# Fetching the rows of expert blocks up to 12 blocks ahead, in two rates, instead of 4 ahead at one a block

## The chip, the core and the metric

The kernel runs on one core of one Trainium2 chip. The metric is the device time in microseconds of one execution, lower is better. TensorE (PE) multiplies matrices and transposes, VectorE (DVE) and ScalarE (ACT) do elementwise work and empty PSUM, GpSimd (POOL) does elementwise work and issues the indirect DMAs, SyncE (SP) issues most of the other DMAs. Each engine works through its own queue in order, and engines wait for one another by semaphores.

## The reference

A transformer block on `x` of 8 x 256 tokens with 256 features, in float32:

```python
x = x + _layernorm(_L0_attn_ref(_layernorm(x), w_qkv, w_o, qn_g, qn_b, kn_g, kn_b))
x = x + _layernorm(_L0_ffn_ref(_layernorm(x), gate_w, w_gate, w_up, w_down, shgate_w, ...))
```

The attention has 16 query heads and 4 key heads of 128, a norm on queries and keys, rotary positions and a causal softmax. The second half, which the change touches, is a mixture of experts:

```python
logits = jnp.einsum('td,ed->te', xf, gate_w)            # 2048 tokens, 8 experts
weights, indices = jax.lax.top_k(softmax(logits), 2)    # two experts a token
g = jnp.einsum('td,edh->teh', xf, w_gate)
u = jnp.einsum('td,edh->teh', xf, w_up)
h = silu(g) * u                                         # 176 hidden units an expert
out = jnp.einsum('teh,ehd,te->td', h, w_down, combine)  # combine: normalised weights
out = out + sigmoid(xf @ shgate_w)[:, None] * (silu(xf @ shw_gate) * (xf @ shw_up) @ shw_down)
```

The last line is a shared expert with 352 hidden units for every token.

## The kernel before, in words

**First half.** Attention runs in a hand-written order over 8 sequences. Tokens are held as 16 tiles of 128. As each tile's attention is done, its normalised rows `xf` are written to a DRAM array `xf_rows`, and its two experts are found. This ends at about 590 us.

**Blocks.** The 2048 x 2 pairs of token and expert are sorted by expert into blocks of 128 rows. There are `NB` = 39 blocks. `load["src"]` holds the row numbers of each block.

**The loop.** `for s in range(CLOSED)` (L1311) is a software pipeline, one slot for each block. In slot `s` the kernel works on four blocks at different stages, in this order on TensorE:

- `turn_block(s)` transposes the fetched rows (`xt`, L1142); VectorE copies the result to `xT` (L1144).
- `open_block(s - 1)` multiplies by the gate and up weights (`gu`, L1158); ScalarE applies silu (`slb`, L1163), VectorE multiplies (`h`, L1165). The expert's number is in a register, loaded for 20 blocks at a time (L1149).
- `close_block(s - 3)` multiplies by the down weights (`py`, L1183); ScalarE copies (`yb`, L1188) and SyncE writes the rows to the DRAM array `ys` (L1189).
- `turn_hidden(s - 2)` transposes the hidden units (`ht`, L1173); ScalarE copies (`hTb`, L1175).

From slot 20 on each slot also holds one step of the shared expert (`gus`, L284, or `sd`, L304), by `fill(1)`.

**Fetches.** `fetch(b)` (L1130) is an indirect DMA on POOL's queue: 128 rows of 1 KB from `xf_rows` into a buffer `xb`. Before, `AHEAD` = 4 blocks are fetched ahead of the loop and slot `s` fetches block `s + 4`. `xb` has five buffers, so the fetch of block `b` waits for the transposes of block `b - 5`.

**Collects.** `collect(i, k)` (L1192) is also an indirect DMA on POOL's queue. It gathers the k-th expert's rows of token tile `i` out of `ys` into `got`. A plan made ahead of the loop puts collects, `combine`, `deviation_of_two` and `leave_tile` into slots. `FULL` = 11, 15, 19, ... 39 is the number of blocks that must be written before a pair of tiles may be collected, so collects begin at slot `FULL[0] + 4` = 15. `combine(i)` (L1202) adds on VectorE what was collected; `deviation_of_two` (L1222) is a small power on POOL (`rstd_d`, L1225) that waits for VectorE and stands in POOL's queue among fetches and collects.

**`places`** (L1086) spreads over slots 2 to 10 some VectorE work (L1103, L1107, L1111) that finds where each token's rows will lie in `ys`.

Of the kernel before, what the change touches and what calls it, by code (L numbers as in the profile page):

```python
# [9 lines left out]
F32 = mybir.dt.float32  # L10
# [9 lines left out]
P = 128  # L20
B, S, HID = 8, 256, 256
# [14 lines left out]
NB = T * TOPK // P + E - 1  # L36
# [6 lines left out]
FULL = [end * TOPK + E - 1 for end in ENDS]  # L43
# [5 lines left out]
def block_kernel(  # L49
# [310 lines left out]
    def fill(n):  # L360
        for f in todo[:n]:
            f()
        del todo[:n]
# [632 lines left out]
    fw = ctx.enter_context(tc.tile_pool(name="fw", bufs=3))  # L996
# [31 lines left out]
    def table():  # L1028

        pn = ps_tr.tile([P, NP], F32, tag="tr", name="total")  # L1030
        nc.tensor.matmul(
            pn, lhsT=ones, rhs=count.rearrange("p g e -> p (g e)"), start=True, stop=True
        )
        n = fc.tile([P, NP], U32, name="n")
        nc.vector.tensor_scalar(n, pn, P - 1.0, None, ALU.add)
        nc.vector.tensor_scalar(n, n, P.bit_length() - 1, None, ALU.logical_shift_right)
        upto = nb[:, E:]
        nc.vector.tensor_copy(upto, n)

        end = fc.tile([P, NP], F32, name="end")  # L1040
        nc.vector.tensor_tensor_scan(
            end, upto, nb[:, :NP], 0.0, ALU.add, ALU.subtract
        )

        off = fc.tile([P, NP], F32, name="off")
        nc.vector.tensor_sub(off, upto, end)
        nc.vector.tensor_add(off, off, lift.rearrange("p g e -> p (g e)"))
        nc.vector.tensor_sub(jump[:, : NP - 1], off[:, 1:], off[:, : NP - 1])

        past = fc.tile([P, NP], F32, name="past")  # L1050
        more = fc.tile([P, 1], F32, name="more")
        nc.vector.scalar_tensor_tensor(
            past, end, part, jump, ALU.is_le, ALU.mult, accum_out=more
        )
        pickT = fc.tile([P, P], F32, name="pickT")
        nc.vector.tensor_scalar(pickT, aside, more, None, ALU.is_equal)
        load["pickT"], load["upto"], load["off"] = pickT, upto, off

    def rows_of():
        ps = ps_tr.tile([P, NB], F32, tag="tr", name="pickp")  # L1060
        nc.tensor.transpose(ps, load["pickT"][:NB, :], ident[:NB, :NB])
        pick = fc.tile([P, NB], F32, name="pick")
        nc.vector.tensor_copy(pick, ps)
        load["pick"] = pick

    def sources():
        ps = ps_tr.tile([P, NB], F32, tag="tr", name="whose")
        nc.tensor.matmul(ps, lhsT=member, rhs=load["pick"], start=True, stop=True)
        src = fc.tile([P, NB], U32, name="src")
        nc.vector.tensor_copy(src, ps)  # L1070
        load["src"] = src
        load["row"] = ps_tr.tile([1, NB], F32, tag="tr", name="row")
        nc.tensor.matmul(load["row"], lhsT=part, rhs=load["pick"], start=True, stop=True)

    def experts():

        er = fc.tile([1, NB], I32, name="er")
        nc.vector.tensor_copy(er, load["row"])
        nc.vector.tensor_scalar(er, er, (T // P).bit_length() - 1, None, ALU.logical_shift_right)
        ei = fc.tile([1, -(-NB // LB) * LB], I32, name="ei")  # L1080
        if ei.shape[1] > NB:
            nc.vector.memset(ei, 0)
        nc.vector.tensor_scalar_min(ei[:, :NB], er, E - 1)
        load["ei"] = ei
# [41 lines left out]

    state = {}
    AHEAD = 4

    def fetch(b):  # L1130
        x_b = fw.tile([P, HID], F32, tag="xb", name=f"xb_{b}", bufs=AHEAD + 1)
        nc.gpsimd.indirect_dma_start(
            out=x_b, out_offset=None, in_=xf_rows,
            in_offset=bass.IndirectOffsetOnAxis(ap=load["src"][:, b : b + 1], axis=0),
        )
        state["x", b] = x_b

    def turn_block(b):
        tr = ps_tr.tile([P, KC, P], F32, tag="tr", name=f"xt_{b}")
        x_b = state.pop(("x", b))  # L1140
        for c in range(KC):
            nc.tensor.transpose(tr[:, c, :], x_b[:, c * P : (c + 1) * P], ident)  # L1142
        xT = fw.tile([P, KC, P], F32, tag="xT", name=f"xT_{b}")
        nc.vector.tensor_copy(xT, tr)  # L1144
        state["xT", b] = xT

    def open_block(b):
        if b % LB == 0:
            _, state["at"] = nc.values_load_multi_w_load_instructions(  # L1149
                load["ei"][:, b : b + LB],  # L1150
                engines=[mybir.EngineType.PE], min_val=0, max_val=E - 1,
                skip_runtime_bounds_check_because="an expert's number, at most 7",
            )
        xT = state.pop(("xT", b))
        gu = ps_mm.tile([P, 2 * HE], F32, tag="mm", name=f"gu_{b}")
        e = state["at"][b % LB]
        for c in range(KC):
            nc.tensor.matmul(  # L1158
                gu, lhsT=xT[:, c, :], rhs=wgu_sb.rearrange("p c (e h) -> p c e h", e=E)[:, c, bass.ds(e, 1), :],
                start=(c == 0), stop=(c == KC - 1),  # L1160
            )
        sl = fw.tile([P, HE], F32, tag="slb", name=f"slb_{b}")
        nc.scalar.activation(sl, gu[:, :HE], AF.Silu)  # L1163
        h = hs[b % 2]
        nc.vector.tensor_mul(h[:, :HE], sl, gu[:, HE:])  # L1165
        state["h", b] = h
        state["e", b] = e
# [81 lines left out]
    def first_share(i):  # L1249
        y = state["y", 0, i]  # L1250
        nc.scalar.activation(y, y, AF.Copy, scale=share[:, i, 0:1])
# [23 lines left out]
    with tc.manual_schedule():  # L1275
        table()
        fill(2)
        rows_of()
        sources()
        for b in range(AHEAD):  # L1280
            fetch(b)
        experts()
        fill(2)

        CLOSED = NB + 3
        plan = {}

        def at(slot, f, *args):
            plan.setdefault(slot, []).append(lambda: f(*args))

        for g in range(G - 3):
            s = FULL[g] + 4
            for j in range(2 * TOPK):
                at(s + j, collect, 2 * g + j // TOPK, j % TOPK)
            for j in range(2):
                at(s + 3 + 2 * j, combine, 2 * g + j)
                at(s + 7 + j, leave_tile, 2 * g + j)
            at(s + 6, deviation_of_two, 2 * g + 1)

        for g in range(G - 3, G - 1):  # L1300
            s = FULL[g] + 4
            for j in range(2 * TOPK):
                at(s + j // TOPK, collect, 2 * g + j // TOPK, j % TOPK)
        g, s = G - 3, FULL[G - 3] + 4
        for j in range(2):
            at(s + 3 + j, combine, 2 * g + j)
            at(s + 6 + j, leave_tile, 2 * g + j)
        at(s + 5, deviation_of_two, 2 * g + 1)
        finding = places()
        LATE = 6  # L1310
        for s in range(CLOSED):  # L1311
            if s + AHEAD < NB:
                fetch(s + AHEAD)
            if s < NB:
                turn_block(s)
            if s == 0:
                fill(1)
            if 0 <= s - 1 < NB:
                open_block(s - 1)
            if 0 <= s - 3 < NB:  # L1320
                close_block(s - 3)
            if 0 <= s - 2 < NB:
                turn_hidden(s - 2)
            if 2 <= s < G + 3:
                next(finding)
            calm = s >= FULL[G - 3] + 7
            if calm:
                for f in plan.pop(s, ()):
                    f()

            if 20 <= s and len(todo) > LATE:
                fill(1)
            for f in plan.pop(s, ()):
                f()
        for f in plan.pop(CLOSED, ()):
            f()
        assert not plan and len(todo) == LATE
        z = NTILES - 4
        for j in range(2 * TOPK):
            collect(z + 2 + j // TOPK, j % TOPK)  # L1340
        fill(2)
        for j in range(2):
            combine(z + j)
        deviation_of_two(z + 1)
        fill(2)
        first_share(z + 2)
        fill(1)
        first_share(z + 3)
        leave_elsewhere(z)
        for j in range(2, 4):  # L1350
            both_shares(z + j)
        fill(1)
        for j in range(2, 4):
            combine_last(z + j)
        for j in range(2, 4):
            leave_last_tile(z + j, (nc.scalar, nc.sync)[j - 2])
        assert not todo
# [47 lines left out]
```

## Time and profile before

| | |
|---|---|
| median of 3 runs | 754.91 us (753.23 to 756.32) |
| profiled execution | 755.46 us |
| its span, first to last instruction | 753.7 us |
| mean granted TensorE clock | 0.988 |
| TensorE busy | 720.3 us, 96% of the span |
| POOL busy | 396.5 us, 53% of the span |
| first fetch issued | 591.59 us |
| last fetch issued | 707.51 us |
| first and last collect issued | 632.23 us, 740.45 us |

Times inside the profiled execution are counted from the start of its span. A row of the timeline gives start, duration, engine, line, operation, output and inputs, and in brackets how long the engine had been idle and what ended that. "issue" means that the profile shows nothing that it waited for. [...]

### The profile page before, as it was taken

How to read it: one execution, taken by the hardware profiler on the slowest of the kernel's cores; microseconds unless marked ns; L12 is line 12 of the kernel's file. 1: busy time of each engine (PE TensorE's matmuls, PEld its weight loads, DVE VectorE, ACT ScalarE, POOL GpSimd, SP SyncE). 2: the span in 40 equal slices, each digit the busy share in tenths (PEclk: the TensorE clock that was granted, in tenths of full speed). 3: DMA queues.
4: the chain of work that ended last, by engine and by line, in shares of the span. 5: the costliest groups of instructions: out<-in, count | busy, mean ns of one | idle time of the engine just before them, and what ended most of it. 6: DMA issues, size and time to landing. Idle time of an engine off the chain costs nothing.

```text
span 753.7 us, 11344 instructions
## 1 busy us (share of the span) xinstructions
PE 720.3 (96%) x3448; PEld 533.8 (71%) x3448; DVE 548.0 (73%) x1464; ACT 459.3 (61%) x1448; POOL 396.5 (53%) x455
## 2 busy tenths in 40 slices
PE   7779999999999999999999999999999899899994
PEld 4446677777777777777777777777887677777773
DVE  4788778788888978896897889678746473354464
ACT  2688877677777767776776767677741333332332
POOL 5568467365546636573654657365212535455423
PEclk9899999999999999999999999999999999999998
DMA  9400000000000000000000000002303133344322
GB/s 309 153 2 1 0 1 8 1 7 1 8 1 7 1 8 8 0 8 1 7 2 8 1 9 7 1 9 70 92 9 91 56 102 119 93 124 116 111 88 76
DMA packets 26915, 32.36 MB, mean 43 GB/s; under 512 B 2980, under 2 KB 23048, under 8 KB 26856
## 3 DMA queue, kind: packets, MB, share of 16 engines
q1 hardware_dynamic: 22752, 21.94, 9.0%
q0 software_dynamic: 3408, 9.31, 4.6%
q8 instruction: 28, 0.46, 0.3%
q10 hardware_dynamic: 696, 0.40, 0.2%
q14 instruction: 31, 0.25, 0.1%
HBM read 22.33 MB, written 9.31 MB: 42 GB/s over the span
## 4 chain that ended last, share of the span: by engine, by line
PE 87%; DVE 4%; ACT 4%; POOL 2%; issue 1%; DMA 1%; SPq 0%; POOLq 0%; DVEq 0%; ACTq 0%
PE qkv L412 20%; PE o L639 15%; PE sc L543 10%; PE av L620 10%; PE gu L1158 6%; PE tp L602 5%; PE py L1183 5%; PE tq L507 4%; PE gus L284 4%; PE sd L304 2%; PE xt L1142 1%; PE ht L1173 1%; ACT qn L454 1%; PE in L768 1%; ACT w_qkv L247 1%
## 5 line engine op out<-in xcount | busy, mean ns | idle before, releaser
L412 PE MATMUL qkv<-w_qkv,xnT 128*128 128x512 f32 x384 | 183.3, 603 | 0.0
L480 POOL TENSOR_TENSOR t<-qn,sg_q 128x256 f32<-128x256 f32 x128 | 118.4, 945 | 54.7 <-ACT qn L454 53.0
L445 POOL TENSOR_TENSOR rstds<-ves,nhalf 128x4 f32<-128x4 f32 x80 | 93.6, 1170 | 74.2 <-DVE ves L436 73.9
L639 PE MATMUL o<-wo_sb,oT 128*128 128x256 f32 x512 | 125.1, 384 | 0.0
L454 ACT ACTIVATE qn<-qkv,rstds 128x128 f32<-128x128 f32 x320 | 91.7, 372 | 33.8 <-POOL rstds L445 33.6
L412 PEld LDWEIGHTS qkv<-w_qkv,xnT 128*128 128x128 f32 x384 | 71.6, 194 | 54.5 <-issue 50.0
L571 ACT ACTIVATE ex<-sc,nmx 128x128 f32<-128x128 f32 (+1 forms) x256 | 105.3, 432 | 5.1 <-DVE nmx L560 4.2
L543 PE MATMUL sc<-kT,q 128*128 128x256 f32 (+1 forms) x512 | 99.7, 328 | 2.5 <-DVE q L517 2.5
L620 PE MATMUL av<-pT,v 128*128 128x256 f32 (+1 forms) x320 | 98.6, 422 | 0.6 <-ACT pT L607 0.6
L639 PEld LDWEIGHTS o<-wo_sb,oT 128*128 128x128 f32 x512 | 91.4, 190 | 9.3
L555 DVE TENSOR_TENSOR sc<-sc,mask 128x256 f32<-128x256 f32 (+1 forms) x96 | 49.3, 514 | 43.1 <-PE sc L543 42.8
L543 PEld LDWEIGHTS sc<-kT,q 128*128 128x128 f32 x512 | 74.7, 191 | 6.0 <-ACT w_qkv L247 2.7
L507 PEld LDWEIGHTS tq<-ident,t 128*128 128x128 f32 x320 | 40.4, 143 | 47.3 <-issue 35.1
L607 ACT COPY pT<-tp 128x512 f32<-128x512 f32 x96 | 57.2, 595 | 24.1 <-PE tp L602 24.1
L560 DVE TENSOR_REDUCE nmx<-sc 128x2 f32<-128x512 f32 (+1 forms) x96 | 66.2, 689 | 2.8
L602 PEld LDWEIGHTS tp<-ident,ex 128*128 128x128 f32 x384 | 47.6, 141 | 25.8 <-issue 12.9
L620 PEld LDWEIGHTS av<-pT,v 128*128 128x128 f32 x320 | 59.0, 190 | 9.2 <-ACT pT L607 1.3
L468 DVE TENSOR_TENSOR t<-qn,cg_q 128x512 f32<-128x512 f32 x64 | 57.9, 904 | 8.5 <-ACT qn L454 8.2
L430 ACT ACTIVATE sq<-qkv 128x512 f32<-128x512 f32 x80 | 48.2, 603 | 22.5 <-PE qkv L412 13.1
L436 DVE TENSOR_REDUCE ves<-sq 128x4 f32<-128x516 f32 x80 | 54.5, 682 | 8.2 <-ACT sq L430 8.0
L602 PE MATMUL tp<-ident,ex 128*128 128x128 f32 x384 | 58.5, 274 | 1.4 <-DVE xnT L402 0.7
L631 ACT COPY oT<-av 128x512 f32<-128x512 f32 x64 | 37.7, 590 | 35.6 <-PE av L620 35.6
(198 smaller groups left out, 1230.1 us busy)
## 6 DMA issues: line engine op xcount, KB each, us to landing
ys<-yb SPq DMA_DIRECT2D x39, 128.0 KB
w_qkv<-in_wqkvT SPq DMA_DIRECT2D x6, 512.0 KB
x_all<-in_x SPq DMA_DIRECT2D x8, 256.0 KB
wo_sb<-in_woT SPq DMA_DIRECT2D x1, 2048.0 KB
xf_rows<-xf SPq DMA_DIRECT2D x16, 128.0 KB
out<-yo SPq DMA_DIRECT2D x14, 128.0 KB
wgu_sb<-in_wg SPq DMA_DIRECT2D x2, 704.0 KB
wgu_sb<-in_wu SPq DMA_DIRECT2D x2, 704.0 KB
```

The costliest lines, as they stand in the source:

```text
L412: nc.tensor.matmul(ps.rearrange("p h d -> p (h d)"), lhsT=seqs[b]["xnT"][t][:, c, :], rhs=w_qkv[g][:, c, :], start=(c == 0), stop=(c == KC ...
L445: nc.gpsimd.tensor_tensor(rstd, now.pop(("ve", b, j)), nhalf, ALU.pow)
L454: nc.scalar.activation(qn[:, h, :], ps[:, h, :], AF.Copy, scale=rstd[:, h : h + 1])
L468: nc.vector.tensor_mul(t1, now["qn", b, j], cg[s][:, t : t + 1, :].to_broadcast([P, REP, D]))
L480: nc.gpsimd.tensor_tensor(t2[:, :, lo : lo + HD], qn[:, :, hi : hi + HD], sg[s][:, t : t + 1, lo : lo + HD].to_broadcast([P, REP, HD]), AL ...
L507: nc.tensor.transpose(tr[:, h, :], t1[:, h, :], ident)
L543: nc.tensor.matmul(sc[:, h, :], lhsT=seqs[b]["qT"][g][:, r0 + h, t * P : (t + 1) * P], rhs=seqs[b]["kT"][:, g, :w], start=True, stop=True,)
L560: nc.vector.tensor_reduce(out=nm, in_=now["sc", b, u], axis=AX.X, op=ALU.max, negate=True)
L571: nc.scalar.activation(ex[:, h, :], sc[:, h, :], AF.Exp, bias=nm[:, h : h + 1], accum_out=rs[:, h : h + 1],)
L602: nc.tensor.transpose(tr[:, c, :], ex[:, h, k * P : (k + 1) * P], ident)
L620: nc.tensor.matmul(now["av"][:, r0 : r0 + nh, :].rearrange("p h q -> p (h q)"), lhsT=seqs[b]["v"][:, k, g * D : (g + 1) * D], rhs=pT[:, k ...
L639: nc.tensor.matmul(now["o", b, t], lhsT=seqs[b]["oT"][h // REP, t][:, h % REP, :], rhs=wo_sb[:, h, :], start=(h == 0), stop=(h == H - 1),)
```

## The change

`AHEAD` stays at 4 and the first four fetches stay ahead of the loop. The buffers of `xb` grow from 5 to 13 (`MOST + 1`). The slot in which a block is fetched now comes from a formula. With `QUIET` = `FULL[0] + 3` = 14, blocks 4 to 24 are put at three in two slots, and later ones at four in seven slots. So slot 0 fetches blocks 4 and 5, slot 10 block 19 only and slot 9 block 18, slot 14 block 25, slot 15 block 26, slot 17 block 27; the last ones are block 36 in slot 33, block 37 in slot 35 and block 38 in slot 36. The most that a fetch runs ahead is 11 slots, the least 2.

```diff
     AHEAD = 4
+    MOST = 12
+    QUIET = FULL[0] + 3
+
+    def slot_of_fetch(b):
+
+        early = QUIET * 3 // 2
+        n = b - AHEAD
+        return n * 2 // 3 if n < early else QUIET + (n - early) * 7 // 4
+
 
     def fetch(b):
-        x_b = fw.tile([P, HID], F32, tag="xb", name=f"xb_{b}", bufs=AHEAD + 1)
+        x_b = fw.tile([P, HID], F32, tag="xb", name=f"xb_{b}", bufs=MOST + 1)
         nc.gpsimd.indirect_dma_start(
...
         for s in range(CLOSED):
-            if s + AHEAD < NB:
-                fetch(s + AHEAD)
+            for b in range(AHEAD, NB):
+                if slot_of_fetch(b) == s:
+                    assert s <= b <= s + MOST
+                    fetch(b)
             if s < NB:
                 turn_block(s)
```

## The prediction

> **What bounds the kernel now.** I read the busy table first, then the windows of the second half, then the list of waits, then the timeline.
>
> ```profile
> PE 720.3 (96%) x3448; PEld 533.8 (71%) x3448; DVE 548.0 (73%) x1464; ACT 459.3 (61%) x1448; POOL 396.5 (53%) x455
> ...
> PE 87%; DVE 4%; ACT 4%; POOL 2%; issue 1%; DMA 1%; SPq 0%; POOLq 0%; DVEq 0%; ACTq 0%
> ```
>
> TensorE is busy for 96% of the span and carries 87% of the chain. A change that leaves its work alone can only act through its gaps. The changed loop starts its first fetch at 591.59 us, so only the last 162 us matter. Windows of 10 us (columns: PE, PEld, DVE, ACT, POOL, clock, DMA share, GB/s):
>
> ```profile
> 590.00:600.00 10.00, 7.67 (x36) 5.65 (x37) 2.78 (x11) 1.33 (x4) 6.58 (x7) 1.00 0.25 73
> 610.00:620.00 10.00, 10.00 (x50) 7.70 (x49) 7.69 (x21) 3.86 (x12) 3.83 (x5) 1.00 0.34 105
> 630.00:640.00 10.00, 10.00 (x49) 7.64 (x48) 2.38 (x7) 2.89 (x9) 6.53 (x7) 1.00 0.44 131
> 640.00:650.00 10.00, 7.88 (x29) 5.69 (x28) 3.77 (x10) 3.07 (x10) 5.68 (x6) 0.83 0.38 115
> ```
>
> TensorE is full except in two of these rows. In 590 to 600 it waits for the first fetch and for its own load of the experts' numbers (1.57 us). In 640 to 650 it loses 2.1 us, and the granted clock is 0.83. Who waited for whom from 590 us on (total, times, longest):
>
> ```profile
> POOL rstd_d L1225 <- DVE mv_d L1220: 25.2, 6, 5.5
> POOL xb L1132 <- PE xt L1142: 21.2, 15, 2.8
> PE xt L1142 <- DMA xb<-xf_rows,src: 0.4, 1, 0.4
> ```
>
> The third line is the one for this change: TensorE waited for a fetched block once, 0.4 us, at the first block. The second is POOL waiting for TensorE to free one of five buffers. No row has VectorE waiting for a `got`. The POOL timeline shows the pace:
>
> ```profile
> 599.40 0.94 POOL L1132 DMA_INDIRECT xb<-xf_rows,src  x1 [0.30 <-issue]
> 600.65 0.95 POOL L1132 DMA_INDIRECT xb<-xf_rows,src  x1 [0.30 <-PE xt L1142]
> ...
> 622.45 0.95 POOL L1132 DMA_INDIRECT xb<-xf_rows,src  x1 [1.54 <-PE xt L1142]
> ...
> 632.23 0.95 POOL L1196 DMA_INDIRECT got<-ys,got  x1 [1.38 <-DVE h L1165]
> 633.48 0.94 POOL L1132 DMA_INDIRECT xb<-xf_rows,src  x1 [0.30 <-PE gu L1158]
> ```
>
> Unhindered, an indirect DMA costs POOL 0.95 + 0.30 = 1.25 us. With five buffers a fetch comes every 2.49 us, the length of a slot before the shared steps are mixed in (`gu` 1.19, `py` 0.86, `ht` 0.22, `xt` 0.22 in the chain). From 632 us a slot issues a fetch and a collect, 2.5 us of POOL in a slot of 2.49.
>
> **The change, part by part.** TensorE, VectorE and ScalarE keep their instructions and their order; only the fetches on POOL's queue move.
>
> *First four fetches and block 0.* The same four are issued ahead of the loop. The first lands 3.06 us after its issue, as before: 0 us.
>
> *Fetches 4 to 26.* The slot formula asks for three in two slots, but POOL's queue knows no slots. A fetch waits only for its buffer, now thirteen deep, so block b waits for the transposes of block b-13. The queue therefore runs at 1.25 us: block 12 at about 606.9 us (before 612.50), block 23 at 620.7. Block 24 meets the transposes of block 11 (621.8), and block 26 those of block 13 (626.8), so it goes at about 627.4 us instead of 657.59. Twenty-five fetches are issued back to back. What this brings: the lead of a fetch over its `xt`, 11.8 us in this stretch, is already near four times the 3.06 us to landing. A longer lead is worth 0.
>
> *Collects.* The first waits for block 10's `ys`, issued at 629.63 us, so it stays at 632.2. Then two collects go per fetch: the fourth collect at about 637.2 us instead of 640.10. Its reader, the combine at slot 20, did not wait for it. Worth 0.
>
> *Fetches 27 to 38.* These come later against their use; the last three run only 3, 2 and 2 slots ahead. They stand behind collects and `rstd_d`, which waits for VectorE. After the `rstd_d` at 705.28 us come two collects, fetch 37 (708.7), two collects, fetch 38 (712.5). With 3.06 us to landing they arrive at 711.8 and 715.6, while their `xt` ran at 718.28 and 722.50. Margins 6.5 and 6.9 us, cost 0. What hides it is that distance; if it were gone, each us late would be a us of TensorE. Behind them the collects of tiles 10 and 11 end one fetch (1.25 us) later than at 713.77 us; they are read from 725 us on: 0.
>
> *VectorE beside the fetches.* In slots 3 to 9 it runs the `places` steps L1103, L1107 and L1111, all with two inputs from SBUF. Their means are 417, 425 and 469 ns; the last coincides with a fetch and is some 0.05 us longer, and fetches there take 0.95 us with one of 1.09. The Trainium skill, "SBUF — State Buffer", section "SBUF: two separate sides", speaks against the change: a VectorE instruction with two SBUF inputs and a GpSimd operation that reads SBUF share one port pair by an exclusive lock, and the loser waits for the whole instruction. By the rule two fetches a slot could hold VectorE for 1.9 us. It is busy 7.69 of 10 us, so 1.91 of a 2.49 us slot with 0.57 spare: 1.3 us over in each of seven slots, +9 us. By the rows two fetches cost about 0.1 us, inside the spare: 0. I take the rows, which show this very overlap, and keep +9 inside the slow case.
>
> *Long runs of indirect DMAs.* Here the trace gives no clean price. Before has five runs of seven from 632 us on, and near the end of each a consumer of TensorE's results starts late without cause. In the first run:
>
> ```profile
> 636.17 0.34 DVE L1165 TENSOR_TENSOR h<-slb,gu 128x176 f32<-128x176 f32 x1 [1.11 <-issue]
> 638.62 0.42 DVE L1144 COPY xT<-xt 128x256 f32<-128x256 f32 x1 [2.10 <-PE gu L1158]
> ...
> 640.75 0.32 ACT L1163 ACTIVATE slb<-gu 128x176 f32<-128x176 f32 x1 [3.42 <-PE gu L1158]
> ...
> 642.88 2.06 PE L1183 MATMUL py<-wd_sb,hTb 128*128 x4 [2.12 <-ACT yb L1188]
> ```
>
> `slb` usually idles 0.97 us, here 3.42: the signal is 2.4 us late, ScalarE's copies follow late, and TensorE idles 2.12 us. From `xt` to `xt` that slot takes 5.96 us (639.19 to 645.15) and the next 3.08 (to 648.23), against 2.49: 3.47 + 0.59 = 4.06 us. The same happens once more: a slot of 5.16 us (692.93 to 698.09) where its chain items sum to 3.79, 1.37 us. In the other three runs the delay stayed inside the slack. The Trainium skill, "TensorE: Matmul & The Clock Gate", section "HAM oscillation — how this bites in real kernels", names only idle gaps over about 3.4 us as what brings the clock down. By it the stall costs its 2.12 us; the row shows 0.83 of clock over 10 us after a gap of 2.12, another 1.7. One more stall is thus +2.1 by the rule and +4.1 by the row; I price by the row.
>
> The bounds: the run of eight at 591.6 to 600.7 us had no such delay, so the new run of twenty-five can cost 0. If one stall comes in every 8 us once `ys` writes run beside it (605 to 622 us), it is two or three, +8 to +12. Below nothing: runs after 632 us are somewhat thinner (six before the first pause instead of seven), and if both present stalls went, -4.06 - 1.37 = -5.4 us. For the likeliest case I take 0, by the nearest row, the eight plain fetches in a row.
>
> **Sum.** 0 + 0 + 0 + 0 + 0 + 0. The profiled execution took 755.46 us (span 753.7 and 1.8 around it), 0.5 above the median of 754.91. I predict 755.0 us.
>
> **The rivals.**
> *Slower: stalls in the long run.* Place: slots 4 to 11 (605 to 622 us), where slots are shortest and the slack of ScalarE and VectorE least. Price 4.06 us a stall; it decides from one stall on if the present ones stay, from two if one of them goes. For it: delays at five run ends of five. Against: none in the run of plain fetches. Two stalls give 763 us, one 759, three 767.
> *Faster: the collect stage stalls less.* For it: fewer fetches between collects. Against: the run from 632 us still has six DMAs, and the first delay came 6 us into it. 755 - 5.4 = 749.6 us.
> *A late fetch at the end.* It needs 6.5 us of delay on POOL; nothing on its queue there waits so long with fetch 37 or 38 still to come. Under 0.03, inside slower.
> *The change doesn't pace as it says.* Certain, and worked in above: the three-in-two rhythm isn't kept by the hardware queue.
>
> **How the numbers follow.** What a measurement of this kernel can tell from no change is about 0.5%, 3.8 us. No change: 0.45 (753 to 758). Slower by over 0.5%: 0.40 (759 to 767). Faster by over 0.5%: 0.15 (749 to 751). The range 750 to 765 leaves out three stalls and the loss of both present ones. The likeliest case's own range is 753 to 758.
>
> **What would show it.** Fetch 26 near 627 us and the first collect still near 632 confirm the movement. A list of waits with `xt` on `xb` of 0.4 us once confirms that leads stay enough. `xt` to `xt` at 2.49 us throughout 605 to 632 us and clock 1.00 there confirm the zero; a slot of 5 us or a clock of 0.83 there is the slow case. Clock 1.00 in the window around 645 us without a new gap is the fast case. Wrong at the root would be a fetch at 2.49 us in the first stretch, or `places` steps near 0.9 us.

## The result, and the profile after

The change makes the kernel slower: 767.46 us (median of 5 runs, 764.07 to 767.69), beside 755.88 us for the kernel before on the same chip (5 runs, 753.23 to 757.00). The ratio is 1.0131, 95% interval 1.0104 to 1.0159. The profiled execution took 767.46 us; its span of 765.7 us is 12.0 us longer than before, and the mean granted clock is 0.98 instead of 0.988.

The busy table of the profile after:

```profile
PE 723.3 (94%) x3448; PEld 535.2 (70%) x3448; DVE 547.9 (72%) x1464; ACT 459.2 (60%) x1448; POOL 396.5 (52%) x455
```

The instruction counts are those of before. TensorE is busy 3.0 us longer with the same work, as the lower clock would have it, so about 9 of the 12 us are new idle time. Windows of 10 us of the kernel after (TensorE, its loads, VectorE, ScalarE, POOL, clock, DMA share, GB/s) show where:

```profile
600.00:610.00 10.00, 5.82 (x27) 3.76 (x25) 1.69 (x6) 0.91 (x3) 7.56 (x9) 0.90 0.36 105
610.00:620.00 10.00, 3.46 (x10) 2.74 (x11) 3.96 (x10) 1.93 (x6) 3.52 (x5) 0.50 0.26 80
620.00:630.00 10.00, 10.00 (x45) 7.37 (x44) 6.07 (x17) 3.21 (x10) 3.53 (x4) 0.91 0.28 89
...
640.00:650.00 10.00, 10.00 (x51) 7.70 (x50) 3.05 (x8) 3.86 (x12) 4.34 (x5) 1.00 0.36 108
```

Between 600 and 620 us TensorE works 9.28 of 20 us, and from about 608 us to 621.7 us the clock is halved (0.90, 0.50 and 0.91 over the first three rows). VectorE and ScalarE are emptier too, so TensorE isn't waiting for a busy engine. The window of 640 to 650 us, which had lost 2.1 us before, is full. The list of waits of the kernel after, from 590 us on (total, times, longest), names the gap:

```profile
ACT slb L1172 <- issue: 12.6, 3, 8.8
PE py L1192 <- ACT hTb L1184: 11.7, 4, 10.6
...
PE xt L1151 <- DMA xb<-xf_rows,src: 0.9, 1, 0.9
```

TensorE waited once for 10.6 us, for ScalarE's copy `hTb`. ScalarE in turn was idle for 8.8 us before one `slb`, and the profile shows nothing that it waited for. No fetched block was late (last line: only the first). The timeline of the kernel after over that stretch:

```profile
602.06 1.05 PE L1167 MATMUL gu<-wgu_sb,xT 128*128 x3
...
604.29 0.44 PE L1151 MATMUL xt<-ident,xb 128*128 128x128 f32 x2
...
604.57 1.35 PE L1167 MATMUL gu<-wgu_sb,xT 128*128 x4
...
610.72 0.95 POOL L1141 DMA_INDIRECT xb<-xf_rows,src  x1 [0.30 <-issue]
610.88 0.32 ACT L1172 ACTIVATE slb<-gu 128x176 f32<-128x176 f32 x1 [8.76 <-issue]
611.24 0.34 DVE L1174 TENSOR_TENSOR h<-slb,gu 128x176 f32<-128x176 f32 x1 [7.00 <-issue]
...
611.98 0.95 POOL L1141 DMA_INDIRECT xb<-xf_rows,src  x1 [0.30 <-issue]
...
615.84 0.37 ACT L1197 COPY yb<-py 128x256 f32<-128x256 f32 x1 [4.64 <-remote]
615.93 0.42 DVE L1153 COPY xT<-xt 128x256 f32<-128x256 f32 x1 [3.04 <-remote]
...
616.16 0.95 POOL L1141 DMA_INDIRECT xb<-xf_rows,src  x1 [3.24 <-remote]
...
616.38 0.34 ACT L1172 ACTIVATE slb<-gu 128x176 f32<-128x176 f32 x1
...
616.54 2.07 PE L1192 MATMUL py<-wd_sb,hTb 128*128 x4 [10.62 <-ACT hTb L1184]
...
622.75 0.38 PE L1151 MATMUL xt<-ident,xb 128*128 128x128 f32 x2
```

And of the kernel before:

```profile
604.07 0.38 PE L1142 MATMUL xt<-ident,xb 128*128 128x128 f32 x2
...
604.49 0.32 ACT L1163 ACTIVATE slb<-gu 128x176 f32<-128x176 f32 x1 [2.33 <-PE xt L1142]
...
609.36 0.38 PE L1142 MATMUL xt<-ident,xb 128*128 128x128 f32 x2
```

In the kernel after TensorE ends its `gu` at 605.92 us and has nothing more that it may do. Which `gu` an `slb` reads follows from the order of the loop. The `slb` at 610.88 reads that of block 2, which ended at 603.11 (602.06 + 1.05); the `gu` that ended at 605.92 is read at 616.38, over 10 us later. The `xt` of block 4 is over at 604.73, and VectorE copies it at 615.93, over 11 us later. ScalarE, VectorE and POOL resume within 0.4 us of one another (615.84 to 616.16), some 3 us after POOL has ended its seventeenth fetch in a row (611.98 + 0.95 = 612.93), and TensorE follows. POOL is hit as well: its eighteenth fetch needs the buffer of block 4, free since 604.73, and starts at 616.16.

So the word that TensorE had finished something reached its consumers late while POOL issued indirect DMAs back to back. It was TensorE's word alone: `h` starts at 611.24, 0.04 us after the `slb` that it reads has ended. The trace also records when an engine raises a semaphore, and it says the same. After 605.92, with no TensorE instruction ending, five raises of TensorE are recorded: one at 613.70 and four from 615.82 to 615.97. A raise of VectorE or ScalarE is recorded, in every run here and until the kernel's end, within 0.15 us of the end of one of its own instructions. The ends of matmuls are modelled in a profile, so that alone does not tell a late word from late work. The clock supports that TensorE was idle: it was halved at 608.07, 2.15 us after 605.92; in the kernel before it was halved at 642.93, 2.17 us after TensorE had fallen idle ahead of 642.88.

From the `xt` of block 4 to that of block 6 pass 18.46 us (604.29 to 622.75); before it was 5.29 (604.07 to 609.36, each kernel's own clock of its span). That is 13.2 us lost in two slots (the gap of 10.62 us, and about 2.6 us in the 5.2 us that TensorE then ran at half clock), and 13.4 by the position of block 6 in the span. From there to the end of the span the kernel after takes 142.95 us and the one before 144.34, so 1.4 us come back: 13.4 - 1.4 = 12.0 us.

### The profile page after: what moved, and what is told of

It is laid out like the page before. It is cut to its first block, busy times and chain, and to the rows that moved or that the text cites. A ratio compares the mean times of both kernels' runs of the same rounds, so it can differ in the third digit from the quotient of the medians.

```text
span 765.7 us, 11342 instructions
## 1 busy us (share of the span) xinstructions
PE 723.3 (94%) x3448; PEld 535.2 (70%) x3448; DVE 547.9 (72%) x1464; ACT 459.2 (60%) x1448; POOL 396.5 (52%) x455
## 4 chain that ended last, share of the span: by engine, by line
PE 86%; ACT 4%; DVE 4%; issue 2%; POOL 2%; DMA 1%; another core or an unknown queue 1%; SPq 0%; POOLq 0%; ACTq 0%; DVEq 0%
PE qkv L412 20%; PE o L639 15%; PE av L620 10%; PE sc L543 10%; PE gu L1167 6%; PE tp L602 5%; PE py L1192 5%; PE tq L507 4%; PE gus L284 4%; PE sd L304 2%; PE xt L1151 1%; PE ht L1182 1%; ACT qn L454 1%; PE in L768 1%; ACT w_qkv L247 1%
## 5 line engine op out<-in xcount | busy, mean ns | idle before, releaser
L591 ACT ACTIVATE ex<-ex,rr 128x256 f32<-128x256 f32 x128 | 58.9, 521 | 0.6 <-DVE rr L579 0.5
```

The source lines that it names most:

```text
L591: nc.scalar.activation(ex[:, h, :], ex[:, h, :], AF.Copy, scale=rr[:, h : h + 1])
```

## The experiments

The theory: runs of row fetches without a pause hold back the signals between engines, and the deeper buffers make the run long. Rivals: the order of the fetches against the collects, DMA traffic, the shared port of VectorE and POOL, the placement of the thirteen buffers. Each group of runs shared a chip, and the kernel before ran beside it.

### First group: which part of the change, and what in it

The kernel before took 755.78 us here (15 runs).

**Slots enforced.** A one-element copy on POOL, reading a tile of the slot before, stands ahead of the fetches of slots 1 to 14:

```diff
+            if 1 <= s <= QUIET:
+                nc.gpsimd.tensor_copy(gate, state["xT", s - 1][0:1, 0, 0:1])
```

> The changed kernel, but in slots 1 to 14 a one-element copy on POOL reads the block transposed in the slot before, ahead of that slot's fetches, so that POOL's queue really goes at three fetches in two slots. Theory A (engines' signals are held back while POOL's indirect DMAs come without a pause, until about 3 us after the last of the run): the longest run is six, no gap of TensorE over 2 us between 598 and 632 us, 752 to 758 us. Theory B (the port that VectorE's two-input instructions share with GpSimd): a fetch rate of 1.5 a slot still meets the places steps, most of the loss stays, 762 us or more. Theory C (traffic of fetched rows beside the ys writes): a part stays, about 760 us. Theory D (the place of thirteen buffers in SBUF and the waits that come with it): 766 us as in the changed kernel.

756.63 us, ratio 1.0003 (0.9986 to 1.0020). The longest run is ten (592.8 to 604.5 us) and not six as expected, and the 10.6 us gap is gone; small gaps stand behind the runs, among them 0.92 us at 606.93. The list of fetches is that of the change, so neither thirteen buffers nor this order costs time by itself. The loss comes from the queue running ahead.

**Buffers alone.** The kernel before with thirteen buffers:

```diff
-        x_b = fw.tile([P, HID], F32, tag="xb", name=f"xb_{b}", bufs=AHEAD + 1)
+        x_b = fw.tile([P, HID], F32, tag="xb", name=f"xb_{b}", bufs=13)
```

> The kernel before, with its order of one fetch a slot, four ahead, but thirteen buffers instead of five. Theory A: POOL's queue is again free to run, seventeen fetches back to back until the fetch that needs the transposes of block 4, the same gap of some 10 us near 604 to 616 us, 764 to 769 us: the buffers do it, not the new order. Were the order of fetches among the slots the cause: 755 us. Theory D: 766 us. Theories B and C: about 766 us.

775.23 us, ratio 1.0246 (1.0200 to 1.0291): worse than the whole change, and 6 us above the expected range. TensorE's timeline in this kernel:

```profile
617.32 2.07 PE L1183 MATMUL py<-wd_sb,hTb 128*128 x4 [10.37 <-ACT hTb L1175]
...
658.70 1.13 PE L1183 MATMUL py<-wd_sb,hTb 128*128 x4 [3.00 <-ACT hTb L1175]
```

The first gap is that of the change, behind the same run of seventeen. The second, and gaps of 3.18 us at 681.7 and 2.73 us at 719.9, stand behind runs of eight, where the queue has more waiting behind each `rstd_d`. One line, the number of buffers, makes the stall.

**Nine buffers** (the change with `bufs=9`). 

> The changed kernel with nine buffers instead of thirteen. Theory A: the first run is four fetches shorter (thirteen instead of seventeen), so it ends 5 us earlier, and so does the gap: about 5 us, 762 us in all (760 to 764). Theory D, and any cause that does not go by the length of the run: 766 us or 755 us, nothing between.

767.25 us, ratio 1.0128 (1.0075 to 1.0181). TensorE's and POOL's timelines in this kernel:

```profile
606.50 0.94 POOL L1141 DMA_INDIRECT xb<-xf_rows,src  x1 [0.30 <-issue]
610.29 0.95 POOL L1141 DMA_INDIRECT xb<-xf_rows,src  x1 [2.84 <-remote]
...
610.79 2.07 PE L1192 MATMUL py<-wd_sb,hTb 128*128 x4 [4.49 <-ACT hTb L1184]
```

The run is thirteen, four more than the buffers, as seventeen is four more than thirteen. It ends 5.5 us earlier than in the change, and the gap is 6.1 us shorter: TensorE resumes 3.4 us after the last fetch here and 3.6 us there. The gap grows with the run, by 6.1 us for four fetches. The time, though, missed the expectation. Block 6 is turned at 617.42 us instead of 622.75, but a gap of 2.21 us at 657.7 with half clock after it, and smaller ones, took that back. They stand behind a run of six collects and fetches; why they came out so much worse here than in the change was not found.

**Rows by SyncE.** Blocks 4 to 38 come as plain DMAs on SyncE's queue, of 128 consecutive rows and not the rows of the block:

```diff
+            nc.sync.dma_start(out=x_b, in_=xf_rows[i * P : (i + 1) * P, :])
```

> The changed kernel, but blocks 4 to 38 are loaded by plain DMAs from SP's queue, 128 consecutive rows of xf_rows each, instead of gathered by POOL: the rows are not those of the block. Same bytes, same buffers, same slots, issued faster. Theory A: no gap, 751 to 757 us. Theory B: no gap either, 751 to 757 us. Theory C: the bytes come denser than before, the gap stays, 764 us or more. Theory D: 766 us.

748.00 us, ratio 0.9882 (0.9838 to 0.9927), under the expected 751 to 757. As many bytes flow: six blocks are issued from 587.3 us on, and from 606.0 us on about three in two slots, among the `ys` writes on the same queue. The windows of this kernel:

```profile
600.00:610.00 10.00, 10.00 (x46) 7.33 (x47) 5.63 (x18) 3.16 (x10) 0.00 (x0) 1.00 0.19 58
610.00:620.00 10.00, 10.00 (x50) 7.69 (x49) 7.49 (x22) 3.86 (x12) 0.00 (x0) 1.00 0.47 138
```

138 GB/s is more than the 80 to 105 of the stalled stretch, and TensorE is full. So neither the amount of traffic nor the placement of the buffers makes the gap. With POOL's fetches gone, the stalls of before go too, and 7.8 us with them; one gap of 1.02 us is left, at 711.0, behind the only run of six collects, while six runs of four cost nothing.

### Second group: no stall to test on

The kernel before took 748.05 us here (47 runs, 746.94 to 750.44). Four kernels ran: the change with a pause on POOL, with plain fetches on POOL, with every slot enforced, and the kernel before with every slot enforced. The edits of the first three are shown in the next group.

> The changed kernel, but POOL clears a scratch tile (a memset of about 1.25 us, used by nobody) after every third fetch from block 6 to 24, so that it is never idle and waits for nothing new, while its indirect DMAs come in threes with a pause. Theory A (signals are held back by indirect DMAs that follow one another without a pause): no gap of several us near 606 us, 754 to 760 us. A rival, that only POOL's waiting for another engine relieves it, or that POOL's being busy is what hurts: 764 us or more.

> The changed kernel, but blocks 4 to 38 are loaded by plain DMAs issued from POOL, 128 consecutive rows of xf_rows each, instead of indirect ones: the rows are not those of the block. If any run of DMAs from POOL's software queue holds the signals back, the gap near 606 us stays, 763 to 770 us. If it takes the reading of an offset for each row: no gap, about 748 us as with SP's queue.

> The changed kernel with the one-element copy ahead of the fetches in every slot from 1 to 38, so that POOL never runs ahead of the slots and no backlog builds up behind rstd_d. Theory A: no run over four past slot 20, the gaps near 646 and 716 us of the first gated kernel go too, 749 to 754 us. If the late gaps come from something else: 755 to 757 us as with the gate in slots 1 to 14 alone.

> The kernel before with the same copy ahead of every slot's fetch. Theory A: the runs of seven behind rstd_d become pairs, the stall near 697 us goes; slots 15 to 19, with two indirect DMAs in 2.5 us, still make a run of ten, so the stall near 640 us stays: 752 to 757 us, and some us over the changed kernel with all gates. If the gates themselves cost: 757 us or more.

They took 749.17, 748.58, 748.99 and 748.62 us, with ratios of 1.0009 (0.9999 to 1.0019), 0.9998 (0.9986 to 1.0010), 1.0010 (0.9998 to 1.0022) and 1.0001 (0.9990 to 1.0013). As tests of the mechanism they decide nothing, because here the kernel before does not stall either. They do show something else: 748 us is reached here without any remedy, the time that the other groups reach only where the stalls are gone. A train of nineteen DMAs with copies between them (591.4 to 616.6 us, in the change with every slot enforced) delayed nobody here. The changed kernel as it stands was not measured in this group.

### Third group: pauses, and the kind of DMA

The stalls are back: the kernel before took 756.46 us (16 runs).

**The change again.** 

> The changed kernel unaltered, to tell which behaviour this chip has: on the chip of the last four runs the kernel before took 748 us and no engine's signal was late, on the chip of the four runs before those it took 756 us. Theory A2 (only on some chips are signals held back while POOL's indirect DMAs follow one another): where before takes 756 us, the changed kernel takes 765 to 769 us with a gap near 606 us; where before takes 748 us, it takes 746 to 751 us without a gap. If the change itself costs 12 us on every chip: 760 us or more beside 748 us.

766.31 us, ratio 1.0120 (1.0090 to 1.0149), a gap of 10.65 us ending at 615.45. The stall repeats.

**Every slot enforced**: the copy of the first experiment in slots 1 to 38. 

> The changed kernel with the one-element copy ahead of the fetches in slots 1 to 38. Theory A2: 749 to 756 us on a chip where before takes 756 us, since no long run is left behind rstd_d; 748 to 750 us on a chip where before takes 748 us. If the gates add work that counts: 2 us or more over before on either chip.

753.51 us, ratio 0.9948 (0.9928 to 0.9968), the first version with every block's own rows that beats the kernel before. Gaps of 0.93 and 1.46 us remain near 605 and 608 us, behind a first run of ten (591.5 to 604.2 us). From 610.2 to 631.2 us fourteen more follow at a mean of 1.61 us from start to start instead of 1.25, and no gap follows them.

**Plain DMAs on POOL.** Blocks 4 to 38 as plain DMAs of consecutive rows:

```diff
+            nc.gpsimd.dma_start(out=x_b, in_=xf_rows[i * P : (i + 1) * P, :])
```

> The changed kernel with blocks 4 to 38 loaded by plain DMAs from POOL, 128 consecutive rows each, not the rows of the block. On a chip where before takes 756 us: 763 to 770 us with a gap near 606 us if any run of POOL's software DMAs holds signals back; 748 to 753 us if it takes the row offsets. On the other kind of chip: 747 to 750 us.

750.05 us, ratio 0.9904 (0.9881 to 0.9926). POOL's timeline and the window of this kernel:

```profile
596.61 0.95 POOL L1142 DMA_INDIRECT xb<-xf_rows,src  x1 [0.30 <-issue]
597.56 7.08 POOL L1148 DMA_DIRECT2D xb<-xf_rows  x13
```

```profile
600.00:610.00 10.00, 10.00 (x49) 7.43 (x48) 5.88 (x18) 3.20 (x11) 5.73 (x11) 1.00 0.68 200
```

Thirteen DMAs go out without a gap and 200 GB/s flow, but nobody waits. So not every run of DMAs on POOL does it. A plain fetch takes POOL 0.55 us and not 0.95, which ends the run of seventeen after 12 us instead of 21. Yet the ten indirect fetches of the kernel with every slot enforced, over 12.7 us in the same group, did leave gaps. So the kind of DMA counts; a run of plain ones for 21 us was not tried.

**A pause in the run.** A memset of 128x1400 on POOL after every third early fetch, nothing else:

```diff
+        if 4 <= b <= 25 and b % 3 == 0:
+            nc.gpsimd.memset(pause, 0.0)
```

> The changed kernel with a memset of about 1.25 us on POOL after every third fetch from block 6 to 24. On a chip where before takes 756 us: 754 to 760 us without a gap of several us near 606 us if a pause between the DMAs is enough; 764 us or more if only POOL's waiting relieves the signals. On the other kind of chip: 747 to 750 us.

756.62 us, ratio 0.9997 (0.9980 to 1.0014). The windows of this kernel:

```profile
600.00:610.00 10.00, 10.00 (x49) 7.57 (x48) 7.00 (x21) 3.65 (x12) 8.46 (x9) 1.00 0.39 117
610.00:620.00 10.00, 10.00 (x50) 7.68 (x49) 7.44 (x20) 3.92 (x13) 8.46 (x9) 1.00 0.43 134
```

POOL is busier than in any other kernel here (8.46 of 10 us), its fetches still run far ahead, and TensorE is full. So POOL's being busy does no harm; 1.29 us without an indirect DMA after every third one is enough. The memset writes to SBUF beside VectorE and costs nothing that can be seen; it reads nothing there, so it does not test the rule on the port that the prediction quotes. The gain stays out because the stage with collects was left alone: behind a run of eight (630.9 to 639.6 us) come gaps of 0.72, 0.79 and 1.49 us, and 1.04 and 0.99 us follow later runs.

### Fourth and fifth group: towards a better kernel

The kernels before took 756.15 and 756.23 us (11 runs each).

**Enforced, and the early fetches one slot later** (`return n * 2 // 3 + 1`). 

> The changed kernel with the one-element copy ahead of the fetches in slots 1 to 38, and the fetches of blocks 4 to 24 one slot later, so that the first run of indirect DMAs shrinks from ten to about seven. Theory A2, on a chip where before takes 756 us: the two gaps left near 605 and 608 us (2.4 us) go, 750 to 752 us, 2 us under the gated kernel of the old order. If those gaps have another cause: 753 to 754 us. On a chip where before takes 748 us: 748 to 750 us.

**Enforced, as above.** 

> The changed kernel with the copy in slots 1 to 38, beside the version with later first fetches on the same chip. 753 to 754 us where before takes 756 us, 748 to 750 us where before takes 748 us.

**The change.** 

> The changed kernel unaltered. Theory A2: 765 to 769 us with a gap near 606 us where before takes 756 us; 746 to 751 us without a gap where before takes 748 us. If the change costs 12 us on every chip: 760 us or more beside 748 us.

752.51 us, ratio 0.9934 (0.9909 to 0.9959); 751.97 us, ratio 0.9941 (0.9920 to 0.9961); 767.87 us, ratio 1.0154 (1.0127 to 1.0181), in this order. The later first fetches gained nothing. The gaps near 605 and 608 us are gone, but one of 2.17 us ending at 636.12 came instead, and the time is 0.5 us above the enforced kernel's, where 2 us under it was expected. The enforced kernel itself came out under its expected range.

**No run over five, as planned.** The copy in every slot from 1 on, and a thinner order: five early fetches in four slots, then one a slot, and the first group's collects in slots with at most one fetch beside them:

```diff
-        early = QUIET * 3 // 2
         n = b - AHEAD
-        return n * 2 // 3 if n < early else QUIET + (n - early) * 7 // 4
+        if n < 18:
+            return 1 + n * 4 // 5
+        return {18: 16, 19: 18}.get(n, n)
...
-                at(s + j, collect, 2 * g + j // TOPK, j % TOPK)
+                at(s + j + (g == 0 and j > 1), collect, 2 * g + j // TOPK, j % TOPK)
...
+            if 1 <= s < NB:
+                nc.gpsimd.tensor_copy(gate, state["xT", s - 1][0:1, 0, 0:1])
```

> Every fetch from slot 1 on is held to its slot by a one-element copy on POOL that reads a tile of the slot before, and the order is thinned: five early fetches in four slots, one per slot later, and the first group's collects in four slots that have no more than one fetch beside them. Theory: with no run of more than about 5 row fetches or collects, no signal is held back, no TensorE gap of over 1 us remains in the block stages, and where the kernel before takes 756 us this takes 749 to 752 us; where the kernel before takes 748 us, no change (747 to 750). Rival (the number of such fetches counts, not the length of a run): no better than the kernel that is gated with the order as it stands, 752 to 754 us.

749.24 us (6 runs, 748.57 to 750.58), ratio 0.9920 (0.9894 to 0.9946). Its windows:

```profile
600.00:620.00 20.00, 20.00 (x97) 15.12 (x96) 13.42 (x38) 7.09 (x23) 12.24 (x20) 1.00 0.37 108
...
640.00:660.00 20.00, 20.00 (x97) 15.78 (x96) 9.38 (x26) 7.19 (x22) 12.30 (x18) 1.00 0.39 118
```

TensorE is full at full clock from 600 to 720 us. All row fetches are still there, in their true order of rows, and the time is that of the kernels without them. Spacing, and not the number of fetches, sets the cost. Some groups came out longer than meant, yet TensorE never idled for them. POOL's timeline of this kernel shows a part of one, seven in 9 us:

```profile
671.58 0.96 POOL L1207 DMA_INDIRECT got<-ys,got  x1 [0.30 <-issue]
672.55 0.27 POOL L1324 COPY gate<-xT 1x1 f32<-1x1 f32 x1
672.98 1.18 POOL L1143 DMA_INDIRECT xb<-xf_rows,src  x1 [0.16 <-issue]
```

The copy between two DMAs widens the pitch a little here. In the kernel with the early fetches one slot later, a run of six at nearly the same pitch (626.7 to 633.3 us), with nine more in threes ahead of it from 612.6 us on, did end in a gap:

```profile
636.12 1.31 PE L1193 MATMUL py<-wd_sb,hTb 128*128 x4 [2.17 <-ACT hTb L1185]
```

So from six or seven on a gap can follow and need not; the runs show no sharp limit.

**The change, a last time.** 

> The changed kernel again, as the control of this chip. Theory (signals held back by long runs of row fetches): where the kernel before takes about 756 us, 765 to 769 us with one TensorE gap of 10 to 11 us near 616 us, behind a run of 17 fetches; where the kernel before takes about 748 us, no such gap and 746 to 751 us. Rival (the faster chips have nothing to do with held-back signals): about 1.3% over the kernel before on every chip.

766.22 us, ratio 1.0143 (1.0109 to 1.0177), one gap of 10.69 us ending at 616.43.

## Why the prediction was wrong

*What bounds the kernel.* Right: TensorE, so that the change can act only through its gaps.

*The queue runs ahead of the formula.* Right in kind, and it is the cause of the loss: the run starts at 591.6 us at 1.25 us a fetch. The length was wrong, 17 instead of 25. The prediction let block 17 take the buffer of block 4 as soon as its transposes were over; that signal came 11 us late, as others of TensorE did. Fetch 26 went at 640.80 us and not at 627, the first collect at 645.69 and not at 632, both because of the stall.

*A longer lead is worth 0.* Right: the wait of `xt` for `xb` is 0.9 us, once. The late fetches were right too: fetches 37 and 38 lead their `xt` by 10.9 and 11.4 us, and nothing waited.

*VectorE beside the fetches.* Taking the rows against the rule on the shared port was right. VectorE runs nothing from 604.23 to 611.24 us, so no instruction of it can have held a port through the stall, and the `places` steps that follow take 0.42 to 0.49 us, as before.

*Long runs of indirect DMAs, costed at 0 by the nearest row.* This step failed. It was put at 0 and measured +13.4 us: TensorE's signals came up to 11 us late. The row it leant on, the eight plain fetches at 591.6 to 600.7 us, was misread: it did have such a delay. In the kernel before the `slb` at 604.49 (shown above, idle for 2.33 us) reads a `gu` that had ended at 603.15, 1.3 us earlier; the next `slb` starts 0.04 us after its `gu`. Five raises of TensorE, of instructions that ended from 603.15 to 604.45, are recorded in one burst from 604.47 to 604.64. The run was short, and TensorE lost only 0.3 us by it (5.29 us for two slots of 2.49). So no row spoke for 0. The rows that spoke against it, five late signals behind five runs of seven, were in the prediction and carried the rival.

*The rival with stalls in the long run.* It named the right mechanism and place (605 to 622 us). Its sum for three stalls, 767 us, was the measured time, but that is luck, for its form was wrong: it took a stall of 4.06 us for every 8 us of run. What came was one backlog. It lasted until 3 us after the run's end, so the gap is about the run's length less eleven microseconds (21.3 us and 10.62 for seventeen fetches, 16.3 and 4.49 for thirteen).

*The clock.* The rule of the Trainium skill, "TensorE: Matmul & The Clock Gate", section "HAM oscillation — how this bites in real kernels", that long idle gaps bring the clock down fits the gap of 10.62 us, with half clock until 621.7 us, although the clock fell only 2.15 us into it. That a shorter gap does it too, as the row of before had shown, was seen again: after the 2.17 us gap at 636.12 the clock was half from 636.9 to 640.4. It need not: after gaps of 3.00 and 2.73 us in the kernel with thirteen buffers (at 658.70 and 719.9) it stayed at 1.00.

*The rival on the collect stage.* Partly right: the present stalls shrank, the 640 to 650 us window is full, and 1.4 us came back. The price of those stalls was undersized. Without them the kernel takes 748 to 750 us on these chips, so they cost about 7 us, not 5.4.

## What to carry to other kernels

A queue that may run ahead does so to the depth of its buffers: the slot in which an instruction is written paces nothing unless something in that slot makes it wait. Deepening a buffer whose loads are never late brings nothing and can turn an even stream into one long run. Where indirect DMAs on POOL come six or more in a row, look at the engines that do not use them: consumers of TensorE's results that idle with no cause shown are the sign, and other work or a gate between the DMAs is the remedy.

## What was not expected of the hardware

Wherever the kernel before took about 756 us (the result and four of five groups), indirect DMAs issued by POOL at 1.25 us each delayed TensorE's signals to the other engines, and not those of VectorE and ScalarE. Runs of four never left TensorE idle; behind runs of six to ten it idles 0.5 to 3.2 us, where it idles at all; behind thirteen 4.49 us, behind seventeen 10.4 to 10.7 us. Behind the two longest kinds the engines resume together, about 3 us after the last DMA of the run. In the second group, where the kernel before took 748 us, nothing of the kind was seen. That group and the fifth carry the same chip number, and in the fifth the stalls were there in full (756.23 and 766.22 us). So, if the number names one and the same chip, it is not a fixed trait of a chip, but a condition that changes between sessions.

What stays open is the reason in the hardware: what sits between an indirect DMA on POOL and a signal from TensorE to ScalarE was not reached by any run here, nor what differed in the second group. One observation bears on it: the traces of the groups with stalls lack records of raised semaphores. TensorE raises its semaphore 733 times in each kernel. The four traces of the second group hold a record of every raise; the others lack 16 to 47 of them, also those of the kernels with plain DMAs, in which TensorE hardly stalls or not at all. Perhaps records and signals share a path that fills up; no run here shows it. All times here were taken with such records being written, and whether the stall is as large without them was not tried, so part of it may belong to the recording.
